# A decoder layer on one core: scale reciprocals moved from GpSimd to ScalarE, a correction product moved to the front of its group, and the second attention unit reordered

## The chip, the core and the metric

The kernel runs on one core of one Trainium2 chip. The metric is device microseconds of one execution. Before the change three runs took 1386.78, 1386.09 and 1386.69 us; the median is 1386.69. One further execution was recorded by the profiler, and every time of a single instruction below is from that record, counted from the start of its span.

The core has five engines with a queue each: PE (matrix products, into PSUM), DVE (VectorE), ACT (ScalarE), POOL (GpSimd) and SP, which here only issues DMAs. An engine works its queue in order. An instruction that waits holds up everything behind it on its engine.

## What is computed

One post-norm decoder layer on x of 8 sequences by 256 tokens by 512:

```python
x = layernorm(x + self_attention(x))        # 16 heads of 128, rotary, causal zeroing; weights sign(s)*exp(|s| - max|s|)
x = layernorm(x + cross_attention(x, ctx))  # 16 heads of 32, scores clipped to +-50, result scaled and normalised
x = layernorm(x + ffn(x))                   # 512 -> 2048 -> 512

def ffn(x):
    h = layernorm(gelu(bitlinear(x, w1, b1)))
    return bitlinear(h, w2, b2)

def bitlinear(x, w, b):
    # s = 127 / max(absmax of the row, 1e-5); xq = clip(round(x * s), -128, 127) / s
    # wq: weights rounded to -1, 0, 1 times their mean magnitude
    return xq @ wq.T + b
```

All of it is float32; the quantised products are made of small integers, times a scale for each row.

## The kernel before

**Self-attention.** The work is 32 units: 8 pairs of heads by 4 pairs of sequences. A float32 product is made of three PE products of a high and a low part (hi·hi, hi·lo, lo·hi: lines L146, L147 and L148). So every x and every weight is loaded into one of three buffers called `raw` and split: the high part is a copy (L156), and the low part a subtraction (L157, or L183 where the halves are made apart). What a unit does is written out by hand as a string of words, `SCHED["unit"]`. A word is one step of the unit's own projections (`Q` and `V` on PE; `w`, `u`, `r`, `R`, `H`, `L` for the rotation: L314 and L315 on ACT, `u` is L320 on DVE, L324 and L332 on POOL, `H` is L341 on ACT, `L` is L348 on POOL or DVE), of the unit before it (`s` to `l`: scores, mask, exponentials `x`, sums `n` and normalising `N`, the last being L411, L412 and the four L419 on DVE), or of the one before that (`o`, `d`: the output product). Other words run background work: `X0` splits the first half of the next unit's x on DVE, `XA` and `XB` make the high and the low part of its second half, `BA`, `BV`, `BW`, `BX`, `BY`, `G0` and `G1` load and split weights. All engines receive the steps in the order of the string; PE's order alone is left to a scheduler after unit 0. The second unit (number 1) has the string with a few replacements, since its predecessor and the loads stand differently: L633 to L637. A `raw` buffer is loaded again only when the split that reads it has run, so the place of `X0` in the string also sets when SP can issue the load of the x after that.

**Cross-attention, its norm and the FFN.** From L640 on the work is a list of steps. Each has an engine (or a choice), a cost and the tiles that it reads and writes; a planner puts the steps in order by these costs, and all queues are emitted in that order. The tokens are 16 tiles of 128. For each tile, after the cross-attention's output product (PE, tile `xo`):

- two norms; `rstd` (L763) makes 1/sqrt(v + eps) from a variance in two POOL instructions, L764 and L765 (the latter with a power of -1/2), and `shift` (L768) on DVE reads it;
- L980 on ACT writes the normed tile; `absmax` (L985 to L987) on DVE finds the row's largest magnitude and the reciprocal of its scale;
- `inverse` on POOL: eight small instructions. L993 writes `a1s`, the row scale that the gelu needs later; L994 clears the fifth block of the quantised tile `xq`; L996 multiplies the reciprocal with the weights' scale, and L999 and L1001 split that number into three bfloat16 parts, which are put into the fifth block (so that the bias can be added by a product);
- L1004 on ACT rounds the tile, by adding and so dropping digits; L1008 on DVE writes it to `xq`;
- SP transposes `xq` by DMA to `xT` (L1010) and stores that; it is loaded back as `xx` (L1060, a DMA that ACT issues) for the first FFN product (`up`, L1070 and L1071 on PE).

The FFN of a tile: the gelu L1075 on ACT, a square for the variance (L1084), three small POOL steps (L1089 to L1091), the second norm in halves (L1103 on ACT, L1105 or POOL for the gamma, L1107 on POOL for the beta, L1108 on DVE), the row's largest magnitude (L1111), then `scale` (L1116 to L1118): the larger of two halves' maxima, its floor and scale, and the reciprocal. ACT or DVE write the quantised `hq` (L1124, L1125), with one half added to make the numbers whole; it is transposed by SP (L1153) or by PE, into `hT`. `down` makes 16 products of 128x512 with `hT` (L1131) and one of a constant with the weights' column sums (L1133), which takes the added half away again. y and the last norm follow (L1155, L764, L765, L768, L1160), and the store.

```python
def down(ks_):
    for k in ks_:
        nc.tensor.matmul(H[dn], H[hT][:, k], H["fw1"][:, 512 * k : 512 * k + 512], start=k == 0, stop=False)
    if 15 in ks_:
        nc.tensor.matmul(H[dn], unhalf, csum, start=False, stop=True)
```

The listing below has the functions that the diff touches.

Of the kernel before, what the change touches and what calls it, by code (L numbers as in the profile page):

```python
# [11 lines left out]
F32R = mybir.dt.float32r  # L12
# [20 lines left out]
EPS = 1e-5  # L33
# [45 lines left out]
def decoder_kernel(ctx: ExitStack, tc: tile.TileContext, a, out):  # L79
# [442 lines left out]
    def background(ui):  # L522
        u = units[ui]
        ex = {k: [] for k in ("B0", "BA", "BV", "BW", "BX", "BY", "XA", "XB", "X0", "X1", "G0", "G1", "BP", "WK", "WV")}
        if ui == 0:
            ex["WK"].append(lambda: load_first("wK"))
            ex["WV"].append(lambda: load_hp(0, "wV", first["wV"]))
        nx = units[ui + 1] if ui + 1 < len(units) else None
        if nx is not None and nx.hp == 0:
            if ui == 0:  # L530
                ex["BA"].append(nx.xload)
            ex["X0" if ui < 2 else "B0"].append(lambda: nx.xsplit(0))
            ex["XA"].append(lambda: x_half(nx.xt, nx.raws[1], 1, 0, nc.scalar))
            ex["XB" if ui > 1 else "X1"].append(lambda: x_half(nx.xt, nx.raws[1], 1, 1, nc.vector))
        elif nx is not None:
            ex["BA"].append(nx.load)
        if ui < 2:
            ex["BV" if ui else "BW"].append(units[ui + 2].xload)
        if u.hp == 0:
            ex["BA" if ui else "X1"].append(lambda: init_acc(u.bp))  # L540
            ex["BA" if ui else "X1"].append(lambda: nc.sync.dma_start(f32(xs[u.bp][:]), f32(u.xt[:])))
        if "wv" in late:
            ex["B0"].append(lambda raw=late.pop("wv"): load_hp(u.hp, "wV", raw["w"]))
        for n, hp, k1 in ([("wO", u.hp, "BW")] if ui else [], [] if ui > 1 else [("wO", 0, "BW")], [("wQ", u.hp + 1, "BW")], [("wK", u.hp + 1, ""), ("wV", u.hp + 1, "")])[u.bp]:
            if (ui or n == "wO") and hp < NHP:
                raws = {}
                ex["BV" if n == "wV" else "BA"].append(lambda n=n, hp=hp, raws=raws: raws.update(w=raw_load(a[n][hp])))
                if n == "wV":
                    late["wv"] = raws
                elif n == "wK":  # L550
                    def hi(raws=raws, hp=hp):
                        w = hw.setdefault(hp, {})["wK"] = T("w", [128, 2, 1024], F32R)
                        half_split(w[:, 0], w[:, 1], raws["w"], 0, nc.scalar)

                    def lo(raws=raws, hp=hp):
                        w = hw[hp]["wK"]
                        half_split(w[:, 0], w[:, 1], raws["w"], 1, nc.vector)

                    ex["G0"].append(hi)
                    ex["BX"].append(lo)  # L560
                else:
                    ex[k1].append(lambda n=n, hp=hp, raws=raws: load_hp(hp, n, raws["w"]))
        if ui in ABS:
            for j in range(2):
                i, rr = 2 * ABS.index(ui) + j, {}
                ex["BA"].append(lambda i=i, rr=rr: rr.update(w=wchunk(i // 8, i % 8)))
                ex[f"G{j}"].append(lambda i=i, rr=rr: wq_abs(rr["w"], i // 8, i % 8))
        if "r2" in late:
# [12 lines left out]
        if ui == len(units) - 2:  # L581
            ex["BA"].append(lambda: kv0.update(wk0r=raw_load(a["wkx"][:, 0:1024])))
            ex["BW"].append(lambda: kv0.update(wk0=split_w(kv0["wk0r"])))
        if ui == len(units) - 1:
            ex["BA"].append(lambda: kv0.update(cr=x_raws(a["ctxT"][0])))

            def ctx_split(i):
                if i == 0:
                    kv0["ctx"] = T("xt", [128, 2, 4, 512], F32R)
                x_split(kv0["ctx"], kv0["cr"][i], i, (nc.vector, nc.gpsimd)[i])  # L590

            ex["X0"].append(lambda: ctx_split(0))
# [38 lines left out]
    for ui, u in enumerate(units):  # L631
        spec = SCHED["unit" if ui else "first"]
        if ui == 1:  # L633
            for old, new in ((" N0 XB", ""), (" n0 m1", " n0 N0 m1"), ("Q000 s00 Q001", "Q000 Q001 s00"), (" S0 BA", " S0 BA f0- f2-"),
                             (" V0 v0", ""), (" t00", " V0 v0 t00")):
                assert old in spec
                spec = spec.replace(old, new, 1)  # L637
# [84 lines left out]
    def new(key):  # L722
        if key in made:
            return []
        made.add(key)
        return [key]
# [127 lines left out]
    def x(b):  # L854
# [80 lines left out]
        for qi in range(2):  # L935
# [29 lines left out]
            def scale1(m1=m1):  # L965
# [12 lines left out]
            S([("POOL-", 1.0, lambda m2=m2: rstd(H[m2]))], wr=[m2])  # L978
# [9 lines left out]

            S([("DVE", 0.85, absmax)], rd=[A], wr=[f"{m2}/s"])

            def inverse(tt=tt, m2=m2, xq=xq):
                s, xq = H[m2], H[xq]
                nc.gpsimd.tensor_tensor(a1s[:, tt : tt + 1], s[:, 10:11], wscale[:, 0:1], ALU.mult)  # L993
                nc.gpsimd.memset(xq[:, 512:640], 0.0)  # L994
                inv = s[:, 12:13]
                nc.gpsimd.tensor_tensor(inv, s[:, 11:12], wscale[:, 2:3], ALU.mult)  # L996
                for n in (3, 2, 1):
                    c0 = 512 + 33 * (3 - n)
                    nc.gpsimd.tensor_copy(xq[:, c0 : c0 + 32 * n - 31 : 32], inv.to_broadcast([128, n]))  # L999
                    if n > 1:  # L1000
                        nc.gpsimd.tensor_tensor(inv, inv, xq[:, c0 : c0 + 1], ALU.subtract)  # L1001

            S([("POOL-", 2.0, inverse)], rd=[f"{m2}/s"], wr=[f"{xq}/i", f"a1s:{tt}"], new=new(xq))
            S([("ACT", 0.71, lambda tt=tt, d=d, m2=m2: nc.scalar.activation(H[d], acc[:, tt], AF.Identity, bias=magic, scale=H[m2][:, 11:12]))],  # L1004
              rd=[A, f"{m2}/s"], wr=[d])
# [44 lines left out]
    def ffn(tt):  # L1050
# [62 lines left out]

        def scale():
            s = H[st]
            nc.vector.tensor_tensor(s[:, 8:9], s[:, 8:9], s[:, 9:10], ALU.max)  # L1116
# [10 lines left out]
        bank(dn)  # L1127

        def down(ks_):
            for k in ks_:  # L1130
                nc.tensor.matmul(H[dn], H[hT][:, k], H["fw1"][:, 512 * k : 512 * k + 512], start=k == 0, stop=False)  # L1131
# [293 lines left out]
```

## Time and profile before

| | |
|---|---|
| median of three runs | 1386.69 us |
| profiled execution | 1387.89 us |
| its span, first to last instruction | 1386.1 us |
| PE busy | 1346.7 us (97%) |
| DVE busy | 1091.8 us (79%) |
| ACT busy | 880.4 us (64%) |
| POOL busy | 782.0 us (56%) |
| mean granted PE clock | 0.992 |
| chain that ended last | PE 82%, DVE 10%, POOL 3%, ACT 2%, issue 2%, DMA 1% |

How to read it: the profiled execution lies 1.8 us above its span, and that part is outside of what the engines do. The busy time of an engine says how full it is over the whole, not in a stage; the table by windows gives the same for one stretch. In a timeline a row has the start, the busy time, the engine, the line, the operation, the tiles that it writes and reads, and, in brackets, the idle time just ahead of it with what ended it. PEclk is the share of the full TensorE clock that was granted.

The stages in time: self-attention to about 900 us, keys, values and cross-attention to about 1225, the FFN from there to the end; FFN products of the first tiles lie between the last tiles of the cross-attention.

### The profile page before, as it was taken

Reading aid. Unit: us, or ns where it says so; the run is one execution under the profiler, and the core shown is the slowest. Engines: PE = TensorE matmul, PEld = TensorE weight load, DVE = VectorE, ACT = ScalarE, POOL = GpSimd, SP = SyncE. Lnnn points to the kernel's source line nnn. Section 1 sums busy time; section 2 is a strip of 40 time slices with the busy share of each in tenths; the row PEclk is TensorE's granted clock in tenths of the full one; section 3 lists DMA queues with packets and bytes.
Section 4 is the critical chain, followed back from the end, with each engine's and each line's share of the span. In section 5 each row is a group of like instructions: output and inputs, shape, how many; then the busy total and the mean of one; then the engine's idle time right before and its main releaser. Section 6 shows DMA issues by size and latency. Waiting matters only on the chain.

```text
span 1386.1 us, 23778 instructions
## 1 busy us (share of the span) xinstructions
PE 1346.7 (97%) x8576; PEld 1081.0 (78%) x8576; DVE 1091.8 (79%) x2040; ACT 880.4 (64%) x1948; POOL 782.0 (56%) x985
## 2 busy tenths in 40 slices
PE   9899999999999999999999999999999999988896
PEld 7789988898889888998889888888667667543342
DVE  6877768778767888887877876868767877798997
ACT  4666776776776666666665666633644445576995
POOL 5656556656666666766665665525033324376764
PEclk9999999999999999999999999999999999999999
DMA  8442342234322244223422342225324424214453
GB/s 309 182 185 109 116 178 107 92 114 165 121 76 96 92 143 176 104 84 124 189 88 99 126 175 107 69 99 191 114 59 126 140 68 143 86 34 94 113 116 99
DMA packets 85046, 170.13 MB, mean 123 GB/s; under 512 B 47040, under 2 KB 57024, under 8 KB 80064
## 3 DMA queue, kind: packets, MB, share of 16 engines
q1 hardware_dynamic: 82624, 165.99, 35.1%
q10 hardware_dynamic: 2304, 2.62, 0.7%
q8 instruction: 68, 1.11, 0.3%
q14 instruction: 50, 0.41, 0.1%
HBM read 130.31 MB, written 27.79 MB: 114 GB/s over the span
## 4 chain that ended last, share of the span: by engine, by line
PE 82%; DVE 10%; POOL 3%; ACT 2%; issue 2%; DMA 1%; SPq 0%; POOLq 0%; ACTq 0%; DVEq 0%
PE ppj L146 12%; PE ppj L147 12%; PE ppj L148 12%; PE pz L146 3%; PE pz L148 3%; PE pz L147 3%; PE pwt L426 3%; PE sc L880 3%; PE den L911 2%; PE av L895 2%; PE ppo L146 2%; PE ppo L147 2%; PE ppo L148 2%; PE psc L376 2%; PE pz L449 2%
## 5 line engine op out<-in xcount | busy, mean ns | idle before, releaser
L324 POOL TENSOR_TENSOR sw<-sw,stab 128x512 f32<-128x512 f32 x128 | 170.2, 1329 | 101.5 <-ACT sw L315 101.0
L146 PE MATMUL ppj<-xt,w 128*128 128x512 f32 x528 | 209.0, 396 | 0.3 <-ACT xt L285 0.3
L147 PE MATMUL ppj<-xt,w 128*128 128x512 f32 x528 | 206.5, 391 | 1.0 <-DVE xt L157 0.4
L148 PE MATMUL ppj<-xt,w 128*128 128x512 f32 x528 | 206.2, 391 | 0.0
L146 PE MATMUL ppj<-w,xt 128*128 128x256 f32 (+1 forms) x528 | 157.2, 298 | 1.1 <-DVE u L320 1.1
L348 POOL TENSOR_TENSOR rh<-u,rh 128x512 fp32r<-128x512 f32 x64 | 97.6, 1526 | 99.8 <-PE ppj L148 88.2
L148 PE MATMUL ppj<-w,xt 128*128 128x256 f32 (+1 forms) x528 | 152.0, 288 | 0.0
L147 PE MATMUL ppj<-w,xt 128*128 128x256 f32 (+1 forms) x528 | 151.9, 288 | 0.0
L320 DVE SCALAR_TENSOR_TENSOR u<-ppj,bqk,ctab 128x512 f32<-128x512 f32 x128 | 95.5, 746 | 70.9 <-ACT sw L315 70.6
L314 ACT ACTIVATE sw<-ppj,bqk 64x512 f32<-64x512 f32 x128 | 87.8, 686 | 92.7 <-PE ppj L148 87.9
L332 POOL TENSOR_TENSOR u<-u,sw 128x256 f32<-128x256 f32 (+1 forms) x128 | 130.8, 1022 | 0.3 <-DVE u L320 0.2
L419 DVE SCALAR_TENSOR_TENSOR e<-aw,rd,sg 128x128 f32<-128x128 f32 (+1 forms) x256 | 126.3, 550 | 0.1
L148 PEld LDWEIGHTS ppj<-xt,w 128*128 128x128 f32 x528 | 99.2, 188 | 21.6 <-DVE w L183 0.4
L406 ACT ACTIVATE aw<-aw,nm 128x256 f32<-128x256 f32 (+1 forms) x256 | 113.2, 443 | 3.9 <-DVE nm L397 3.9
L391 POOL TENSOR_SCALAR_AFFINE_SELECT aw<-aw 128x256 f32<-128x256 f32 x128 | 59.9, 492 | 98.7 <-ACT aw L385 98.7
L453 ACT CAST z<-pz 128x512 fp32r<-128x512 f32 x64 | 37.6, 587 | 121.3 <-PE pz L449 121.3
L147 PEld LDWEIGHTS ppj<-xt,w 128*128 128x128 f32 x528 | 99.3, 188 | 17.9 <-DVE xt L183 0.8
L146 PEld LDWEIGHTS ppj<-xt,w 128*128 128x128 f32 x528 | 99.3, 188 | 17.1 <-ACT xt L285 0.7
L146 PEld LDWEIGHTS ppj<-w,xt 128*128 128x128 f32 x528 | 101.9, 193 | 2.0 <-DVE u L320 1.4
L147 PEld LDWEIGHTS ppj<-w,xt 128*128 128x128 f32 x528 | 102.0, 193 | 0.6
L148 PEld LDWEIGHTS ppj<-w,xt 128*128 128x128 f32 x528 | 101.7, 193 | 0.7
L385 ACT ACTIVATE aw<-psc 128x384 f32<-128x384 f32 x128 | 62.3, 487 | 60.6 <-PE psc L148 59.9
(283 smaller groups left out, 3937.0 us busy)
## 6 DMA issues: line engine op xcount, KB each, us to landing
xt<-xs SPq DMA_DIRECT2D x28, 2048.0 KB, 8.2
xs<-xt SPq DMA_DIRECT2D x4, 2048.0 KB, 12.9
raw<-w1T SPq DMA_DIRECT2D x16, 512.0 KB, 9.5
raw<-w2T SPq DMA_DIRECT2D x16, 512.0 KB, 9.6
acc<-xn SPq DMA_DIRECT2D x4, 1024.0 KB, 8.5
raw<-wO SPq DMA_DIRECT2D x8, 512.0 KB, 9.6
wq<-wqt SPq DMA_DIRECT2D x16, 256.0 KB, 2.4
kx<-ks SPq DMA_DIRECT2D x8, 512.0 KB, 4.9
```

The lines of the kernel that those rows point to most:

```text
L146: nc.tensor.matmul(ps, lh, rh, start=first, stop=False)
L147: nc.tensor.matmul(ps, lh, rl, start=False, stop=False)
L148: nc.tensor.matmul(ps, ll, rh, start=False, stop=last)
L314: nc.scalar.activation(sw[0:64], ps[64:128], AF.Identity, bias=bias[64:128])
L320: nc.vector.scalar_tensor_tensor(v3(u), v3(self.ps.pop((h, i))), self.bias(h, i), ctab.to_broadcast([128, 2, 256]), ALU.add, ALU.mult)
L324: nc.gpsimd.tensor_tensor(v3(sw), v3(sw), stab.to_broadcast([128, 2, 256]), ALU.mult)
L332: nc.gpsimd.tensor_tensor(u, u, sw, ALU.add)
L348: (nc.gpsimd if i else nc.vector).tensor_tensor(lo, u if i else u[:, :, 128:256], f32(hi), ALU.subtract)
L385: nc.scalar.activation(aw[:, h], sc3, AF.Abs, scale=1.0 / math.sqrt(DH))
L391: nc.gpsimd.affine_select(aw[:, :, blk], aw[:, :, blk], pattern=[[0, 2], [-1, 128]], compare_op=ALU.is_ge, fill=MASKED, base=0, channel_mu ...
L406: nc.scalar.activation(aw[:, h, blk], aw[:, h, blk], AF.Exp, bias=nm[:, h, i : i + 1], accum_out=rd[:, h, i : i + 1])
L419: nc.vector.scalar_tensor_tensor(e[:, h, blk], aw[:, h, blk], rd[:, h, i : i + 1], sg[:, h, blk], ALU.mult, ALU.mult)
```

## The change

Six edits:

1. The seven small POOL instructions of `inverse` (all but the clearing) become seven small ACT instructions, emitted right behind the rounding L1004. The clearing of `xq`'s fifth block stays on POOL and moves to the step of `rstd`. The planner's POOL step remains as an empty one with its cost, and the ACT step keeps the cost 0.71, so the order of all other work is as before.
2. `rstd`'s first instruction multiplies by 1.0 and adds epsilon, where it only added.
3. `scale` takes the maximum by an instruction with one tensor and a pointer to the other number, with the floor in it; the product with 1/127 is the next one.
4. `down` makes the correction product first.
5. Unit 1 has other replacements: `X0` goes from behind `R00` to behind `N1`; `x0` goes ahead of `H00`; `N0` and the second `u10` go ahead of `R01`, and `L00` behind `N0`; `XA` and `XB` come later (`XB` at `BY`).
6. In unit 1 the weight wO is split in two steps, the high part on ACT at `G1` and the low part on DVE at `BW`, where DVE did both at `BW`.

```diff
-            ex["XB" if ui > 1 else "X1"].append(lambda: x_half(nx.xt, nx.raws[1], 1, 1, nc.vector))
+            ex["XB" if ui > 1 else "BY" if ui else "X1"].append(lambda: x_half(nx.xt, nx.raws[1], 1, 1, nc.vector))
...
-                elif n == "wK":
+                elif n == "wK" or ui == 1:
...
-                    ex["G0"].append(hi)
-                    ex["BX"].append(lo)
+                    ex["G0" if n == "wK" else "G1"].append(hi)
+                    ex["BX" if n == "wK" else "BW"].append(lo)
...
-            for old, new in ((" N0 XB", ""), (" n0 m1", " n0 N0 m1"), ("Q000 s00 Q001", "Q000 Q001 s00"), (" S0 BA", " S0 BA f0- f2-"),
+            for old, new in ((" N0 XB", ""), (" L00 n0 m1", " n0 N0 L00 u10 m1"), (" H01 u10 R10", " H01 R10"), (" H00 x0 a11 XA", " x0 H00 a11"), (" R00 X0", " R00"), (" N1 X1", " N1 X0"),
+                             (" l0 k10 k11 BX", " XA l0 k10 k11 BX"), ("Q000 s00 Q001", "Q000 Q001 s00"), (" S0 BA", " S0 BA f0- f2-"),
...
-        nc.gpsimd.tensor_scalar(mv[:, 2:3], mv[:, 1:2], EPS, None, ALU.add)
+        nc.gpsimd.tensor_scalar(mv[:, 2:3], mv[:, 1:2], 1.0, EPS, ALU.mult, ALU.add)
...
+            def rstd_zero(m2=m2, xq=xq):
+                rstd(H[m2])
+                nc.gpsimd.memset(H[xq][:, 512:640], 0.0)
...
-            def inverse(tt=tt, m2=m2, xq=xq):
-                s, xq = H[m2], H[xq]
-                nc.gpsimd.tensor_tensor(a1s[:, tt : tt + 1], s[:, 10:11], wscale[:, 0:1], ALU.mult)
-                nc.gpsimd.memset(xq[:, 512:640], 0.0)
+            S([("POOL-", 2.0, lambda: None)], rd=[f"{m2}/s"], wr=[f"{xq}/i", f"a1s:{tt}"], new=new(xq))
+
+            def rounded(tt=tt, d=d, m2=m2, xq=xq):
+                s, s_xq = H[m2], H[xq]
+                nc.scalar.activation(H[d], acc[:, tt], AF.Identity, bias=magic, scale=s[:, 11:12])
                 inv = s[:, 12:13]
-                nc.gpsimd.tensor_tensor(inv, s[:, 11:12], wscale[:, 2:3], ALU.mult)
-                for n in (3, 2, 1):
-                    c0 = 512 + 33 * (3 - n)
-                    nc.gpsimd.tensor_copy(xq[:, c0 : c0 + 32 * n - 31 : 32], inv.to_broadcast([128, n]))
+                nc.scalar.activation(inv, s[:, 11:12], AF.Identity, scale=wscale[:, 2:3])
+                for c0, n in ((512, 3), (545, 2), (578, 1)):
+                    nc.scalar.copy(s_xq[:, c0 : c0 + 32 * n - 31 : 32], inv.to_broadcast([128, n]))
                     if n > 1:
-                        nc.gpsimd.tensor_tensor(inv, inv, xq[:, c0 : c0 + 1], ALU.subtract)
-
-            S([("POOL-", 2.0, inverse)], rd=[f"{m2}/s"], wr=[f"{xq}/i", f"a1s:{tt}"], new=new(xq))
...
+                        nc.scalar.activation(inv, s_xq[:, c0 : c0 + 1], AF.Identity, scale=-1.0, bias=inv)
+                nc.scalar.activation(a1s[:, tt : tt + 1], s[:, 10:11], AF.Identity, scale=wscale[:, 0:1])
+
+            S([("ACT", 0.71, rounded)], rd=[A, f"{m2}/s"], wr=[d])
...
-            nc.vector.tensor_tensor(s[:, 8:9], s[:, 8:9], s[:, 9:10], ALU.max)
-            nc.vector.tensor_scalar(s[:, 8:9], s[:, 8:9], EPS, 1.0 / 127.0, ALU.max, ALU.mult)
+            nc.vector.tensor_scalar(s[:, 8:9], s[:, 8:9], s[:, 9:10], EPS, ALU.max, ALU.max)
+            nc.vector.tensor_scalar(s[:, 8:9], s[:, 8:9], 1.0 / 127.0, None, ALU.mult)
...
+            if 0 in ks_:
+                nc.tensor.matmul(H[dn], unhalf, csum, start=True, stop=False)
             for k in ks_:
-                nc.tensor.matmul(H[dn], H[hT][:, k], H["fw1"][:, 512 * k : 512 * k + 512], start=k == 0, stop=False)
-            if 15 in ks_:
-                nc.tensor.matmul(H[dn], unhalf, csum, start=False, stop=True)
+                nc.tensor.matmul(H[dn], H[hT][:, k], H["fw1"][:, 512 * k : 512 * k + 512], start=False, stop=k == 15)
```

More of the change, by code (lines that the diff above doesn't have):

```diff
@@ L549, in background, with hi, lo @@
                     late["wv"] = raws
-                elif n == "wK":
-                    def hi(raws=raws, hp=hp):
-                        w = hw.setdefault(hp, {})["wK"] = T("w", [128, 2, 1024], F32R)
+                elif n == "wK" or ui == 1:
+                    def hi(raws=raws, hp=hp, n=n):
+                        w = hw.setdefault(hp, {})[n] = T("w", [128, 2, 1024], F32R)
                         half_split(w[:, 0], w[:, 1], raws["w"], 0, nc.scalar)
-                    def lo(raws=raws, hp=hp):
-                        w = hw[hp]["wK"]
+                    def lo(raws=raws, hp=hp, n=n):
+                        w = hw[hp][n]
                         half_split(w[:, 0], w[:, 1], raws["w"], 1, nc.vector)
-                    ex["G0"].append(hi)
-                    ex["BX"].append(lo)
+                    ex["G0" if n == "wK" else "G1"].append(hi)
+                    ex["BX" if n == "wK" else "BW"].append(lo)
                 else:
@@ L977, in x @@
                ("ACT", 2.1, lambda d=d, m2=m2, xq=xq: astats(H[d], H[m2], H[xq][:, 0:512]))], rd=[d], wr=[m2, f"{xq}/q"], new=[m2] + new(xq))
-            S([("POOL-", 1.0, lambda m2=m2: rstd(H[m2]))], wr=[m2])
+            def rstd_zero(m2=m2, xq=xq):
+                rstd(H[m2])
+                nc.gpsimd.memset(H[xq][:, 512:640], 0.0)
+            S([("POOL-", 1.0, rstd_zero)], wr=[m2])
             S([("DVE", 0.13, lambda m2=m2: shift(H[m2]))], wr=[m2])
@@ L989, in x @@
             S([("DVE", 0.85, absmax)], rd=[A], wr=[f"{m2}/s"])
-            def inverse(tt=tt, m2=m2, xq=xq):
-                s, xq = H[m2], H[xq]
-                nc.gpsimd.tensor_tensor(a1s[:, tt : tt + 1], s[:, 10:11], wscale[:, 0:1], ALU.mult)
-                nc.gpsimd.memset(xq[:, 512:640], 0.0)
+            S([("POOL-", 2.0, lambda: None)], rd=[f"{m2}/s"], wr=[f"{xq}/i", f"a1s:{tt}"], new=new(xq))
+            def rounded(tt=tt, d=d, m2=m2, xq=xq):
+                s, s_xq = H[m2], H[xq]
+                nc.scalar.activation(H[d], acc[:, tt], AF.Identity, bias=magic, scale=s[:, 11:12])
                 inv = s[:, 12:13]
-                nc.gpsimd.tensor_tensor(inv, s[:, 11:12], wscale[:, 2:3], ALU.mult)
-                for n in (3, 2, 1):
-                    c0 = 512 + 33 * (3 - n)
-                    nc.gpsimd.tensor_copy(xq[:, c0 : c0 + 32 * n - 31 : 32], inv.to_broadcast([128, n]))
+                nc.scalar.activation(inv, s[:, 11:12], AF.Identity, scale=wscale[:, 2:3])
+                for c0, n in ((512, 3), (545, 2), (578, 1)):
+                    nc.scalar.copy(s_xq[:, c0 : c0 + 32 * n - 31 : 32], inv.to_broadcast([128, n]))
                     if n > 1:
-                        nc.gpsimd.tensor_tensor(inv, inv, xq[:, c0 : c0 + 1], ALU.subtract)
-            S([("POOL-", 2.0, inverse)], rd=[f"{m2}/s"], wr=[f"{xq}/i", f"a1s:{tt}"], new=new(xq))
-            S([("ACT", 0.71, lambda tt=tt, d=d, m2=m2: nc.scalar.activation(H[d], acc[:, tt], AF.Identity, bias=magic, scale=H[m2][:, 11:12]))],
-              rd=[A, f"{m2}/s"], wr=[d])
+                        nc.scalar.activation(inv, s_xq[:, c0 : c0 + 1], AF.Identity, scale=-1.0, bias=inv)
+                nc.scalar.activation(a1s[:, tt : tt + 1], s[:, 10:11], AF.Identity, scale=wscale[:, 0:1])
+            S([("ACT", 0.71, rounded)], rd=[A, f"{m2}/s"], wr=[d])
             S([(e, us, lambda tt=tt, g=g: g.tensor_tensor(acc[:, tt], acc[:, tt], H["b2b"], ALU.add))
```

## The prediction, made before the changed kernel had run

> **What bounds the kernel now.** I read the table by windows first, because the page's 97% for PE is a mean over stages with different limits.
>
> ```profile
> core 0: us, PE busy (x) PEld busy (x) DVE busy (x) ACT busy (x) POOL busy (x), PEclk, DMA share, GB/s
> 0.00:40.00 40.00, 36.52 (x189) 30.28 (x190) 26.50 (x44) 18.29 (x31) 22.69 (x24) 1.00 0.85 306
> 40.00:80.00 40.00, 36.17 (x205) 31.59 (x204) 32.48 (x60) 29.39 (x80) 26.96 (x29) 0.91 0.33 119
> 80.00:900.00 820.00, 819.68 (x5023) 732.87 (x5022) 644.64 (x1222) 545.97 (x1435) 516.17 (x541) 1.00 0.33 124
> 1200.00:1250.00 50.00, 43.77 (x250) 23.30 (x242) 43.11 (x81) 34.90 (x51) 31.27 (x63) 0.93 0.16 40
> 1250.00:1300.00 50.00, 41.91 (x179) 17.72 (x179) 43.87 (x75) 36.89 (x44) 33.43 (x41) 0.93 0.46 102
> 1300.00:1350.00 50.00, 47.39 (x219) 21.08 (x218) 49.31 (x89) 48.41 (x60) 33.80 (x43) 1.00 0.53 115
> ```
>
> From 80 to 900 us PE is busy 819.68 of 820 us (and 298.33 of 300 from 900 to 1200): whatever is gained before 80 us is kept, and whatever ACT, DVE or POOL spares inside is worth nothing unless a PE row waits for it. The places to gain are the two stretches with PEclk 0.91 and 0.93, and the end, where DVE is busy 49.31 of 50. DVE's own waits from 1276 to 1373 sum to 0.9 us, so DVE time saved there counts in full.
>
> Unit 1 is the first stretch. In PE's timeline the fourth column is the idle time before a row and its releaser:
>
> ```profile
> 44.05 0.33 PE L426 MATMUL pwt<-ident,e 128*128 128x128 f32 x1 [1.57 <-DVE e L419]
> 44.59 0.44 PE L426 MATMUL pwt<-ident,e 128*128 128x128 f32 x2 [0.21 <-DVE e L419]
> 45.86 0.83 PE L426 MATMUL pwt<-ident,e 128*128 128x128 f32 x3 [0.83 <-DVE e L419]
> 47.84 0.58 PE L146 MATMUL ppj<-w,xt 128*128 128x256 f32 x1 [1.15 <-DVE u L320]
> 48.22 0.42 PE L147 MATMUL ppj<-w,xt 128*128 128x256 f32 x1
> ```
>
> PE waits 1.57 + 0.21 + 0.83 + 1.15 = 3.76 us for DVE, and then its clock falls: 26 matmuls of 256 columns start 0.214 us apart, against 0.119 elsewhere, (0.214 - 0.119) x 26 = 2.5 us more. The stretch loses 6.3 us. DVE is late because it splits unit 2's x just before; its subtraction L157 is stretched:
>
> ```profile
> 36.40 0.86 DVE L156 CAST xt<-raw 128x1024 fp32r<-128x1024 f32 x1
> 37.30 2.20 DVE L157 TENSOR_TENSOR xt<-raw,xt 128x1024 fp32r<-128x1024 f32 x1
> 39.42 0.74 DVE L320 SCALAR_TENSOR_TENSOR u<-ppj,bqk,ctab 128x512 f32<-128x512 f32 x1
> ```
>
> The second place is the start of the FFN. The chain of waits there:
>
> ```profile
> 1247.98 1.27 POOL a1s L993
> ...
> 1249.76 0.56 POOL xq L999
> ...
> 1250.39 1.19 POOL mb L1001
> ...
> 1252.16 0.20 POOL xq L999
> 1252.38 2.57 DMA xT<-xq
> 1254.97 0.32 SPq L1011
> 1255.39 4.32 DMA hT<-hq
> 1259.75 6.37 PE dn L1131 x16
> ...
> 1274.12 2.12 DVE fs L1116
> ```
>
> POOL's tiny operations on 128x1 take up to 1.27 us instead of 0.19. The last release the xT transposes on SP, the first hT transpose waits in SP's queue behind them, and PE is idle 4.77 us before dn, which then runs at half clock (6.37 us, against 3.63 at 1375.69).
>
> **Unit 1 reordered.** X0 (0.86 + 2.20 on DVE) leaves its place ahead of L320 of u01 (39.42) and goes behind N1; the second u10 comes before R01; L00 goes behind N0. Walking the new order with each row's own duration: u01 at 37.7 (not 39.42), H00 39.5, the four L419 39.95 to 42.25 (before 43.45 to 46.2), u10 42.55 to 43.25 (before 47.05 to 47.78). The projection that started at 47.84 can start at 43.3. What is late next: its second group wants L348 of L01 on POOL, about 47.0 (1.55 us idle); the third waits for u11 (0.5); unit 2's first projection waits for X0, now 52.2 to 54.1 (0.45), and XB's subtraction, now behind w's high half, 56.15 to 57.4 (0.7); with small ones of 1.0 that is 4.2 us idle, but spread over 15 us. The 12th matmul of unit 2 ends at 58.5 instead of 61.1: **-2.6 us**. Bounds: if the clock falls anyway, +1.7, so -0.9; if the L348 wait vanishes too, -6. A loss is possible by one DMA: unit 3's first raw load needs X0's buffer, so its issue on SP moves from 39.52 to 54.2. Its landing took 3.8 us then and 7.3 to 11.4 for other raw loads of the stage; it lands at 58 to 65.6, wanted by DVE at about 60. Behind it in SP's queue stand the second raw load, acc, xs and wQ, none wanted before 70. At worst 5 us are lost here, net +2.5.
>
> wO's high half goes from DVE (0.68) to ACT (1.04): the walk holds it, and ACT has 10 us idle of 40 there.
>
> **Reciprocals to ACT.** Each of 16 tiles takes seven small operations off POOL (0.32 + 0.30 + 0.28 + 0.31 + 0.31 + 0.31 + 0.28 = 2.1 us mean, 2.5 with gaps) and puts seven behind L1004 on ACT. L758 to L761 show a small ACTIVATE at 0.19 to 0.20, and a pointer operand at 0.1 (L757 0.62 with none, L759 0.72 with one, L1004 0.82 with two). Four with one pointer, three without, six of them dependent with 0.04 between: 4 x 0.29 + 3 x 0.19 + 6 x 0.04 - overlap of the last, 0.2 = 1.7 us. I take **1.6 per tile**; bounds 1.3 (no pointer price) and 2.0. No table is loaded for it.
>
> What stands behind them on ACT decides. The place to read it is tile 5:
>
> ```profile
> 1103.58 0.82 ACT L1004 ACTIVATE d<-acc,magic,mb 128x512 f32<-128x512 f32 x1 [1.19 <-DVE mb L987]
> 1104.31 0.67 ACT L845 ACTIVATE qst<-qp,bqx 128x512 f32<-128x512 f32 x1
> 1104.88 1.93 ACT L884 ACTIVATE pt<-sc 128x1024 f32<-128x1024 f32 x2
> ```
>
> L845 starts as L1004 ends, the two exps follow it, and the score matmuls L880 at 1106.73 have 0.05 us of slack to them: PE loses up to 1.6. Tile 7 has 0.86 us of ACT idle behind it and then an exp with 0.29 of slack (loss 0.5); tile 9, 0.2. Tiles 0, 1, 6 and 8 have gaps of 1.31 to 4.63 us; tiles 2 and 4 have PE slacks of 1.45 and 1.48 against delays of 0.8 and 1.4. So 1.6 + 0.5 + 0.2 = 2.3, less some slack that returns: **+2.0**, bounds 0 and +5 (a delay passing on through PE at tiles 2, 4, 10 and 11 too).
>
> At the FFN, ACT is full from 1238.8 to 1249.3, so tile 15's L1004 moves from 1247.36 to 1248.9 (1.6 for tile 14's burst before it), its parts are ready at 1251.1, not 1252.36, and xT, hT and dn come 1.2 us earlier. L1107 (two times 2.4 us on POOL, now from 1252.31 because the tiny operations stand before it) can start near 1246; DVE's wait of 3.04 at 1251.6 goes with it, but what it feeds waits for ACT's gelus, 1.6 late each. I take **-1.5** for both, bounds +3.2 (two bursts in full) and -5.
>
> **L1116.** The two-operand max took 2.19 us at 1274.04, against a median of 0.15, because POOL's L1107 ran from 1272.88 to 1276.21. In that same time DVE's L768, one operand with a pointer, took 0.20 at 1273.91. The new max has L768's form: 2.19 - 0.16 = **-2.0** at a point from where DVE is saturated. Bounds 0 (still held) and -2.7 (with the 0.65 at 1234.51).
>
> The Trainium skill, "SBUF — State Buffer", section "SBUF: two separate sides", says that a VectorE instruction with two SBUF inputs and a GpSimd one lock each other out for a whole instruction. By that rule the new form runs free whenever POOL runs; L768's 0.20 agrees. The same rule would free DVE from the seven operations on POOL as well, and nothing in my sum counts that. The skill's "ScalarE: Activation LUTs", section "What ACT_TABLE_LOAD costs", speaks against the change: 186 ns for an ACTIVATE and 93 more per pointer operand, so by estimate 4 x 0.28 + 3 x 0.19 = 1.69 us a tile, where my sum has 1.6; by the page the tile 5 loss would be 0.1 more.
>
> **down and rstd.** The correction product goes ahead of the 16 matmuls that wait for hT; the last of these releases y instead of L1133 (1379.32, 0.23 us). Other tiles are DVE-bound: **-0.3**, bounds 0 and -1. rstd keeps its instructions (L764 0.33, L967 with two operations 0.36): 0, bounds ±0.3. The moved memset (0.2) stays on POOL behind L765, and delays DVE's shift by nothing, as that waits for L765 alone.
>
> **Sum**, against the profiled 1387.89 us (span 1386.1 and 1.8 around it): -2.6 + 2.0 - 1.5 - 2.0 - 0.3 = -4.4, giving 1383.5. The profiled execution is 1.2 above the median, so 1386.69 - 4.4 = **1382.3** on the median's scale.
>
> **The rivals.**
> - Larger gain: the idle in unit 1 is spread, so the clock stays up and L348 comes sooner (-5), the FFN's start gives its best (-5), the middle costs 0.5: -10 to -12, about 1376. For it: every loss I named rests on slacks under 1.6 us. Against: POOL is already 27 of 40 busy in unit 1.
> - No change: the clock falls in unit 1 (-0.9), the middle costs 3, L1116 is held by another POOL operation (-1), the start of the FFN gives -1: about 0, 1386.7.
> - **Slower**: ACT becomes the bound at the FFN's start. Tiles 12 to 15 each put 1.6 us into ACT's queue, which has 1.35 us of idle behind tile 13's L1004 and none from 1238.8 to 1249.3; if gelu L1075 releases DVE and PE last, 4 x 1.6 - 1.35 = 5 us come in, DVE's saturated stretch starts later by 5 - 1.5, and with +2 in the middle, -2.6 from unit 1 and nothing else gained it is +3: 1390. It decides once the gelus delay dn more than the earlier transposes advance it, that is over 2.7 us. Against it: hT's transpose, not a gelu, released PE at 1259.75.
>
> **How the numbers follow.** About 0.2% (2.8 us) is what a measurement of this kernel tells from no change. Chances: forecast 0.46 (1379 to 1383.9), larger gain 0.16, no change 0.19, slower 0.19. So faster 0.62, same 0.19, slower 0.19. The forecast, the no-change case and most of the larger gain must be inside for 8 in 10, and the unknown bounds reach both: 1375.5 to 1388.5.
>
> **What would show it.** Right: PE's 47.84 row at 43 to 44 us and 256-column matmuls 0.12 apart; L1116 all at 0.2; xT's last landing and dn near 1251 after the shift, DVE busy over 49 of 50 to the end. Wrong: PE idle behind L884 of 0.5 us or more at more than three tiles; a DMA as releaser at 60 us; PE's wait before the first dn above 4.8 us with an ACT row as its releaser.

## The result, and the profile after

The changed kernel takes 1394.14 us (median of 6 runs, 1393.39 to 1394.68), against 1386.74 for the kernel before in its 6 runs: a ratio of 1.0053, interval 1.0040 to 1.0066. It is slower by some 7.4 us. Its profiled execution took 1393.39 us with a span of 1391.5. The forecast was 1382.3, with 1388.5 as the upper end.

Line numbers of the changed kernel lie one higher at L764 to L975 (L802 is L803), four or five higher around the rounding (L980 is L985, L1006 is L1010; the rounding itself, L1004, is L1000) and four in most of the FFN (L1060 is L1064, L1107 is L1111, L1116 is L1120). The kernels of the experiments have numbers of their own, off by a few lines; the names of the tiles tell the rows.

Where it went is read by stage. To make the two traces comparable I follow PE's instructions, which come in the same order in both but for the first stage, and note by how much each starts later than before. The shift is -1.1 to -1.3 us from unit 2 to 960 us, -1.7 from 990 to 1056, +0.6 after 1058, +2.1 after 1108, +2.5 after 1150, +2.9 at 1204; then comes the FFN's start, with almost +9 at its worst, and +5.4 is left at the end. The table by windows has the same (the columns are those of the table in the prediction):

```profile
core 0: us, PE busy (x) PEld busy (x) DVE busy (x) ACT busy (x) POOL busy (x), PEclk, DMA share, GB/s
...
1000.00:1100.00 100.00, 98.09 (x820) 68.88 (x821) 73.99 (x136) 51.59 (x99) 28.14 (x46) 1.00 0.31 98
1100.00:1200.00 100.00, 98.35 (x897) 65.93 (x899) 70.51 (x131) 60.34 (x114) 23.81 (x44) 1.00 0.38 116
1200.00:1250.00 50.00, 41.05 (x264) 22.99 (x265) 42.07 (x79) 38.94 (x77) 23.39 (x38) 0.97 0.12 31
```

PE was busy 100.00 and 99.72 of the first two windows before; it now has 1.9 and 1.6 us of idle time in a stage where all of it counts. ACT went from 44.39 and 54.36 to 51.59 and 60.34, and POOL from 36.62 and 36.61 to 28.14 and 23.81: the move happened as planned, and neither engine is near full.

The stall near 1057 us. The kernel before comes first, with a DVE, a POOL and a PE row; the bracket is the idle time ahead of the row and what ended it:

```profile
1053.07 0.69 DVE L985 TENSOR_REDUCE mb<-acc 128x1 f32<-128x512 f32 x1 [0.28 <-ACT acc L980]
...
1055.42 0.69 DVE L785 CAST ctx<-cr 128x1024 fp32r<-128x1024 f32 x1
1056.43 0.69 DVE L802 TENSOR_TENSOR kvs<-kvp,bvb 128x512 f32<-128x512 f32 x1 [0.33 <-POOL mb L1001]
```

```profile
1056.63 1.27 POOL L1006 TENSOR_TENSOR acc<-acc,b2b 128x512 f32<-128x512 f32 x1
```

```profile
1057.34 0.50 PE L146 MATMUL kvp<-w,ctx 128*128 128x512 f32 x1
```

The changed kernel, DVE, POOL and PE:

```profile
1053.17 0.69 DVE L990 TENSOR_REDUCE mb<-acc 128x1 f32<-128x512 f32 x1 [2.05 <-ACT acc L985]
...
1055.53 1.75 DVE L786 CAST ctx<-cr 128x1024 fp32r<-128x1024 f32 x1
1057.20 0.68 DVE L803 TENSOR_TENSOR kvs<-kvp,bvb 128x512 f32<-128x512 f32 x1
```

```profile
1055.23 1.50 POOL L1010 TENSOR_TENSOR acc<-acc,b2b 128x512 f32<-128x512 f32 x1 [2.95 <-ACT d L1000]
```

```profile
1057.93 0.50 PE L146 MATMUL kvp<-w,ctx 128*128 128x512 f32 x1 [1.91 <-DVE kvs L803]
```

Two things delay L803, which frees a PSUM bank for PE. ACT's L985 of the next tile stands behind a burst, so DVE waits 2.05 us where it waited 0.28. And the cast L786, now beside POOL's L1010, takes 1.75 us; before, it took 0.69 here and at 1048.22. PE, which did not wait here before, waits 1.91.

The stall near 1107 us is the one that the prediction named (tile 5), first on ACT, then on PE. Before, the score products ran without a wait:

```profile
1106.73 1.26 PE L880 MATMUL sc<-qst,kx 32*128 32x256 f32 x16
```

In the changed kernel:

```profile
1104.62 0.28 ACT L1002 ACTIVATE mb<-mb,wscale 128x1 f32<-128x1 f32 x1
...
1106.20 0.29 ACT L1007 ACTIVATE a1s<-mb,wscale 128x1 f32<-128x1 f32 x1
1106.39 0.67 ACT L846 ACTIVATE qst<-qp,bqx 128x512 f32<-128x512 f32 x1
1106.96 1.93 ACT L885 ACTIVATE pt<-sc 128x1024 f32<-128x1024 f32 x2
```

```profile
1108.03 0.70 PE L881 MATMUL sc<-qst,kx 32*128 32x256 f32 x4 [0.64 <-ACT pt L885]
```

From L1002 to L846 it is 1.77 us: the seven. PE comes out 1.5 us later.

At the FFN's start the chain of waits no longer goes through POOL's tiny operations. It goes through ACT's burst and then through two DVE rows, and by several short steps to a load of xx:

```profile
1249.99 0.82 ACT acc L985
...
1254.49 2.75 DVE acc L1010
...
1257.31 3.22 DVE h L1112
...
1269.08 3.21 DMA xx<-xqs
...
1272.34 1.89 PE up L1074 x4
```

PE waits 5.16 us for that load. L985 is again the next tile's norm behind a burst. L1010 and L1112 are ordinary additions, which took 0.67 and 1.27 us before. POOL's pair of additions lies beside them. It starts later than before (1252.31), because it waits for a DVE row that stands behind L985:

```profile
1254.23 5.21 POOL L1111 TENSOR_TENSOR h<-h,be 128x1024 f32<-128x1024 f32 x2 [3.75 <-DVE h L1109]
```

### The profile page after: what moved, and what is told of

The parts are those of the page before. It is cut to its first block, busy times and chain, and to the rows that moved or that the text cites. A ratio compares the mean times of both kernels' runs of the same rounds, so it can differ in the third digit from the quotient of the medians.

```text
span 1391.5 us, 23789 instructions
## 1 busy us (share of the span) xinstructions
PE 1347.6 (97%) x8564; PEld 1080.5 (78%) x8576; DVE 1093.8 (79%) x2039; ACT 905.2 (65%) x2061; POOL 750.7 (54%) x873
## 5 line engine op out<-in xcount | busy, mean ns | idle before, releaser
L348 POOL TENSOR_TENSOR rh<-u,rh 128x512 fp32r<-128x512 f32 x64 | 97.5, 1523 | 98.3 <-PE ppj L148 88.2
L419 DVE SCALAR_TENSOR_TENSOR e<-aw,rd,sg 128x128 f32<-128x128 f32 (+1 forms) x256 | 127.1, 554 | 0.1
```

Of the source, the lines that this page charges most:

```text
L348: (nc.gpsimd if i else nc.vector).tensor_tensor(lo, u if i else u[:, :, 128:256], f32(hi), ALU.subtract)
L419: nc.vector.scalar_tensor_tensor(e[:, h, blk], aw[:, h, blk], rd[:, h, i : i + 1], sg[:, h, blk], ALU.mult, ALU.mult)
```

## The experiments

The theories, stated before the first of them. **A, burst**: the seven ACTIVATEs hold up what stands behind them on ACT. **B, collision**: POOL, with the small work gone, runs its large additions sooner, at times when DVE needs the same memory. **C**: another of the edits costs it. The kernel before was timed again beside each; its median was 1386.9 to 1387.6.

**All edits but the first.**

```diff
-            S([("POOL-", 2.0, lambda: None)], rd=[f"{m2}/s"], ...)   # and the seven in rounded()
+            S([("POOL-", 2.0, inverse)], rd=[f"{m2}/s"], ...)        # as before
```

> All edits but the first: the seven small operations of a tile are POOL's again. Theory A (burst): the seven ACTIVATEs behind the rounding hold up what stands behind them on ACT, about 1.6 us a tile, and cost some 9 us; the rest of the change gains 1 to 2.5. Theory B (collision): POOL, freed of the seven, runs its 128x512 and 128x1024 operations at times when DVE needs the same memory, and this costs the 9 us. Theory C: another edit (the correction product first, the new maximum) costs it. A and B: 1384 to 1386. C: 1390 or more.

1384.99 us, ratio 0.9985 (0.9975 to 0.9994). C falls: the rest of the change is a gain of about 2 us.

**The first edit alone**, that is the hunks on `rstd_zero`, `inverse` and `rounded`.

```diff
-            S([("POOL-", 2.0, inverse)], rd=[f"{m2}/s"], ...)
+            S([("POOL-", 2.0, lambda: None)], rd=[f"{m2}/s"], ...)   # and the seven in rounded()
```

> The kernel before with the first edit alone (seven small operations of a tile from POOL to ACT). A and B: 1394 to 1397, PE waiting about 2.0 us near 1057 us and 1.5 near 1107, as in the changed kernel. C: 1386 to 1388.

1396.60, ratio 1.0067 (1.0052 to 1.0082): 9.6 us more. With the gain of the rest that makes 7.6, beside the 7.4 of the whole change. PE waits 1.9 us for L802 near 1057 and 0.8 for the exponentials, as in the changed kernel.

**POOL freed, burst left out.** Against the kernel with the first edit alone:

```diff
                 nc.scalar.activation(H[d], acc[:, tt], AF.Identity, bias=magic, scale=s[:, 11:12])
-                inv = s[:, 12:13]
-                nc.scalar.activation(inv, ...)   # and the three copies and two differences
                 nc.scalar.activation(a1s[:, tt : tt + 1], s[:, 10:11], AF.Identity, scale=wscale[:, 0:1])
```

> The kernel before with POOL freed, but ACT gets one small operation a tile (the row scale for the gelu) and not seven: the three bfloat16 parts of the reciprocal are left out, so the FFN's first bias is not added. POOL is as free as in the changed kernel, ACT's burst is 0.3 us and not 1.7. A: 1385 to 1388. B: 1391 or more, with the cast of ctx at 1057 us stretched to 1.7 us and PE waiting behind it.

1390.07, ratio 1.0021 (1.0011 to 1.0031): 3.0 us more, between the two expectations. One ACTIVATE of 0.28 us a tile is still on ACT, so the 3.0 is the freed POOL's cost together with that one's.

**Burst added, POOL not freed.**

```diff
                 nc.scalar.activation(H[d], acc[:, tt], AF.Identity, bias=magic, scale=s[:, 11:12])
+                a_, b_ = s[:, 13:14], s[:, 14:15]
+                nc.scalar.activation(a_, s[:, 11:12], AF.Identity, scale=wscale[:, 2:3])
+                for n in (3, 2, 1):
+                    nc.scalar.copy(b_, a_)
+                    if n > 1:
+                        nc.scalar.activation(a_, b_, AF.Identity, scale=-1.0, bias=a_)
+                nc.scalar.activation(s[:, 15:16], s[:, 10:11], AF.Identity, scale=wscale[:, 0:1])
```

> The kernel before, with seven more small ACTIVATEs of the same kinds behind each rounding, written to unused columns; POOL keeps its own seven. ACT has the burst and POOL is not freed. A: 1393 to 1396. B: 1386 to 1389. If each has a part: both this and the kernel without the parts lie between 1387 and 1393, and their excesses add up to that of the first edit alone.

1393.14, ratio 1.0046 (1.0031 to 1.0061): 6.1 us more. So A is the larger part by the medians, B is real, and 6.1 + 3.0 = 9.1 beside the 9.6 of both together. The place near 1057 us shows the two apart. DVE with the burst alone:

```profile
1053.04 0.69 DVE L985 TENSOR_REDUCE mb<-acc 128x1 f32<-128x512 f32 x1 [1.99 <-ACT acc L980]
...
1055.38 0.69 DVE L785 CAST ctx<-cr 128x1024 fp32r<-128x1024 f32 x1
```

DVE with POOL freed alone, and POOL beside it:

```profile
1051.65 0.69 DVE L989 TENSOR_REDUCE mb<-acc 128x1 f32<-128x512 f32 x1 [0.47 <-ACT acc L984]
...
1054.01 1.77 DVE L785 CAST ctx<-cr 128x1024 fp32r<-128x1024 f32 x1
```

```profile
1053.72 1.52 POOL L1003 TENSOR_TENSOR acc<-acc,b2b 128x512 f32<-128x512 f32 x1 [1.38 <-ACT d L999]
```

The burst gives the wait and a cast of 0.69. Freed POOL gives hardly a wait, but its addition, which before began 1.2 us after the cast did, now lies over it, and the cast takes 1.77. PE waits 0.8 us in the one, 0.6 in the other, and 1.9 with both. At the FFN's start the same is seen larger. DVE before, then with POOL freed alone, then POOL in that kernel:

```profile
1249.58 0.67 DVE L1006 TENSOR_TENSOR acc<-acc,b2b 128x512 f32<-128x512 f32 x1
1250.25 1.27 DVE L1108 SCALAR_TENSOR_TENSOR h<-h,fs,be 128x1024 f32<-128x1024 f32 x1
...
1254.68 2.35 DVE L1111 TENSOR_REDUCE fs<-h 128x1 f32<-128x1024 f32 x2 [3.04 <-POOL h L1107]
```

```profile
1249.33 2.85 DVE L1003 TENSOR_TENSOR acc<-acc,b2b 128x512 f32<-128x512 f32 x1
1252.17 3.30 DVE L1105 SCALAR_TENSOR_TENSOR h<-h,fs,be 128x1024 f32<-128x1024 f32 x1
```

```profile
1249.16 5.23 POOL L1104 TENSOR_TENSOR h<-h,be 128x1024 f32<-128x1024 f32 x2 [2.42 <-DVE h L1102]
```

POOL's pair of additions starts at 1249.16, not 1252.31: 3.1 us sooner, half of the some 6 that were forecast. But DVE's two additions now lie beside it and pay 2.18 + 2.03 = 4.2 us, and what DVE saves is its wait of 3.04.

A freed POOL is not the only way to such a meeting. With the burst alone DVE comes later to the second addition, and there it meets POOL's pair too, first the DVE row, then the POOL row:

```profile
1254.17 3.43 DVE L1119 SCALAR_TENSOR_TENSOR h<-h,fs,be 128x1024 f32<-128x1024 f32 x1
```

```profile
1254.18 5.62 POOL L1118 TENSOR_TENSOR h<-h,be 128x1024 f32<-128x1024 f32 x2
```

So 6.1 and 3.0 tell the two edits apart, but not waiting from collision: part of the burst's 6.1 is a collision as well.

**Where on the way: the first twelve tiles, and the last four.** The first edit is made for one part of the tiles only.

```diff
+            if tt < 12:      # tt >= 12 in the other
+                S([("ACT", 0.71, rounded)], ...)                   # the seven on ACT
+            else:
                 S([("POOL-", 2.0, inverse)], ...)                  # the seven on POOL
```

> The kernel before with the first edit at the tiles 0 to 11 alone (those that lie beside the cross-attention's products, where PE is busy throughout); the last four tiles keep the seven operations on POOL. The prediction's share for these tiles: 2.0 more, 1389.5. By the trace of the first edit alone, PE is 6.1 later at 1201 us than before: if that is kept to the end, 1393 to 1394; if the waits of the FFN's start (10 us of idle PE in 1226 to 1260) absorb it, 1388 to 1390.

> The kernel before with the first edit at the tiles 12 to 15 alone, those that the FFN's start waits for. The prediction's share for these: 1.5 less, 1386.0. If the burst holds up the next tile's norm on ACT and the gelus here, and POOL's 128x1024 additions meet DVE's two-tensor operations: 2.5 to 5 more, 1390 to 1392.5. The two shares add up to the 9.6 of the whole edit if neither absorbs the other.

1393.15, ratio 1.0044 (1.0029 to 1.0059), 6.3 us more; and 1389.93, ratio 1.0022 (1.0012 to 1.0031), 3.1 us more. Together 9.4: the shares add up, and nothing of a delay from before the FFN is absorbed at its start. In the first of them PE's waits from 1226 us on are those of before (hT 10.2 us, xx 7.3), only later. Its trace also shows what a wait can draw after it. PE's shift grows by 6.2 us from 1054 to 1225, against 4.7 in the changed kernel's trace. Both have the wait of 1.91 at 1057. But with the first twelve tiles alone the granted clock is then 0.72 from 1057 to 1063 (that is 3.4 us at half clock), against 1.00 in the changed kernel, and PE loses 1.6 us more there. The trace of the first edit alone has that spell too (0.74). In how many of the other executions it came, the record doesn't show.

**The same burst, later on ACT.** It is emitted with the step of L1012.

```diff
-            S([("ACT", 0.71, rounded)], ...)    # rounding and the seven
+            S([("ACT", 0.71, rounded)], ...)    # rounding
...
+            S([("DVE+", 0.36, store)], ...)     # L1012's step, and the seven on ACT
```

> The changed kernel with the same seven ACTIVATEs a tile, emitted with the step that stores the quantised tile, so that one to three other ACT instructions of the same plan go ahead of them: the next tile's norm at the second and third tile (near 1057 us), an exponential or the next scale elsewhere, a gelu at the FFN's start; at the tile near 1107 us the exponentials stay behind them. If the cost is in what stands behind the burst: PE's wait near 1057 falls from 1.9 to the 0.6 that the freed POOL alone shows, the 1.5 near 1107 stays, 1389 to 1392.5. If 1.6 us more on ACT cost the same wherever they stand: 1393 to 1395.

1392.65, ratio 1.0036 (1.0024 to 1.0048). Near 1057 PE waits 0.85 and not 1.91; near 1107 it still loses 1.5; against the kernel before it is 5.1 us more, where the changed kernel is 7.4, a difference that the two intervals do not separate. The places moved as A says; the sum says little.

**xx loaded by SP**, since ACT issued one such load at 1249.61, behind a burst, and PE waited 5.1 us for it.

```diff
-        S([("SP", 0.9, lambda: nc.scalar.dma_start(H[x2], xqs[tt]))], ...)
+        S([("SP", 0.9, lambda: nc.sync.dma_start(H[x2], xqs[tt]))], ...)
```

> The changed kernel with the loads of xx issued by SP, not ACT. In the changed kernel ACT issues the load at 1249.61 behind a burst, and PE waits 5.1 us for it. If that is what makes the FFN's start late: 3 us or more less, 1391 or below. If the start is late by ACT's queue itself (the next tile's norm L985 behind the burst, DVE behind that): within 1.5 of the changed kernel's 1394, though PE's wait for xx is another.

1393.88, ratio 1.0045 (1.0032 to 1.0059): 6.3 us more, no gain that the intervals tell from the changed kernel's 1.0053. PE's wait at that place falls to 0.3 us and comes back at the next (3.0, 2.9). Who issues the load was not what made the stage late.

**The seven on DVE**, at the end of the step with the row's maximum, and none on ACT.

```diff
                 nc.vector.reciprocal(s[:, 11:12], s[:, 10:11])
+                nc.vector.tensor_scalar(inv, s[:, 11:12], wscale[:, 2:3], None, ALU.mult)
+                for c0, n in ((512, 3), (545, 2), (578, 1)):
+                    nc.vector.tensor_copy(s_xq[:, c0 : c0 + 32 * n - 31 : 32], inv.to_broadcast([128, n]))
+                    if n > 1:
+                        nc.vector.tensor_tensor(inv, inv, s_xq[:, c0 : c0 + 1], ALU.subtract)
+                nc.vector.tensor_scalar(a1s[:, tt : tt + 1], s[:, 10:11], wscale[:, 0:1], None, ALU.mult)
```

> The changed kernel with the seven small operations on DVE, at the end of the step that finds the row's maximum, and none on ACT. POOL is freed as in the changed kernel. ACT's burst is gone and its 6 us with it; what the freed POOL costs (3 us) stays, and DVE gets some 1.4 us a tile. If DVE hides them as ACT could not, since it has 26 of 100 us idle from 1000 to 1200: 1386 to 1389. If a burst of this length hurts on any engine ahead of the copies that PE waits for: 1391 to 1396.

1397.13, ratio 1.0070 (1.0056 to 1.0084): 9.6 us more, no better than on ACT. In the changed kernel DVE has 26 us idle of 100, but here PE waits for its masked exponentials, its kvs, rs and cT (0.3 to 0.7 us at five places before 1201 us; it is 4.5 later there), and the FFN's start adds 5 more. An idle quarter is no cover when what PE needs next stands right behind.

**The order planned anew.**

```diff
-            S([("POOL-", 2.0, lambda: None)], ...)
...
-            S([("ACT", 0.71, rounded)], rd=[A, f"{m2}/s"], wr=[d])
+            S([("ACT", 2.3, rounded)], rd=[A, f"{m2}/s"], wr=[d, f"{xq}/i", f"a1s:{tt}"], new=new(xq))
```

> The changed kernel, with the planner told of the burst: the empty POOL step is gone, and the rounding step has a cost of 2.3 instead of 0.71, so the order of all engines behind it is planned anew. If the burst hurts by standing ahead of exponentials, gelus and loads that an ignorant plan put right behind it, a plan that knows it gets half of it or more back: 1385 to 1390. If the 1.6 us a tile on ACT hurt wherever they stand: 1392 to 1396.

1502.06, ratio 1.0825: neither. The new plan changes between exponentials and gelus, with 8 loads of a function table at 1.28 us each where there were 2, and PE waits 32 us for hT. It tells how much the order of the plan is worth, and nothing on the burst.

**The other edits one by one**, each with the kernel before around it. First the maximum.

```diff
-            nc.vector.tensor_tensor(s[:, 8:9], s[:, 8:9], s[:, 9:10], ALU.max)
+            nc.vector.tensor_scalar(s[:, 8:9], s[:, 8:9], s[:, 9:10], EPS, ALU.max, ALU.max)
```

> The kernel before with the new maximum alone. L1116 takes 0.2 us everywhere. The prediction's step: DVE is the bound from there on, so 2.0 us less, 1385.0. Rival: DVE comes to y 2 us sooner and waits there for the second dn, whose time its transpose and PE set: 0 to 0.6 less, 1386.4 to 1387.0.

1385.66, ratio 0.9988 (0.9979 to 0.9996). The row that took 2.19 us before, with POOL's addition beside it as it was before:

```profile
1272.24 0.20 DVE L1116 TENSOR_SCALAR fs<-fs 128x1 f32<-128x1 f32 x1
```

```profile
1271.09 3.35 POOL L1107 TENSOR_TENSOR h<-h,be 128x1024 f32<-128x1024 f32 x1 [1.65 <-DVE h L1105]
```

The second unit (edits 5 and 6 of the list).

```diff
-            for old, new in ((" N0 XB", ""), (" n0 m1", " n0 N0 m1"), ...)
+            for old, new in ((" N0 XB", ""), (" L00 n0 m1", " n0 N0 L00 u10 m1"), ...)
```

> The kernel before with the second unit reordered and wO split in two steps, nothing else. The prediction's step: 2.6 us less, 1384.4 against 1387.0. What the changed kernel's trace says (0.7 us less idle, a half-clock stretch shorter by part of a window, which differs between executions by itself): 0.5 to 1.3 us less, 1385.7 to 1386.5.

1386.58, ratio 0.9995 (0.9986 to 1.0004): 0.8 us less, not told from no change.

The correction product and `rstd` (edits 4 and 2).

```diff
+            if 0 in ks_:
+                nc.tensor.matmul(H[dn], unhalf, csum, start=True, stop=False)
```

> The kernel before with the correction product first and the other form of the variance's first step. The prediction's step: 0.3 us less, 1386.7. If the sum of the edits is what the kernel without the parts shows (2.0 less), the three parts of it, this one, the new maximum and the second unit, add up to 2.0.

1386.49, ratio 0.9994 (0.9986 to 1.0003): 0.8 less, not told from no change either; by the traces DVE's rows lie 0.2 us sooner than before at 1200 and 0.5 sooner from 1282 on. The three together make 3.3, with intervals of some 1.2 each, beside the 2.0 of the kernel that has all three.

**A shorter chain on POOL**, with all edits but the first.

```diff
             def rstd_zero(m2=m2, xq=xq):
                 rstd(H[m2])
+                nc.gpsimd.memset(H[xq][:, 512:640], 0.0)      # out of inverse
...
                         nc.gpsimd.tensor_tensor(inv, inv, xq[:, c0 : c0 + 1], ALU.subtract)
+                nc.gpsimd.tensor_tensor(a1s[:, tt : tt + 1], s[:, 10:11], wscale[:, 0:1], ALU.mult)   # was first
```

> The kernel with all edits but the first, with the clearing of the fifth block moved to the step of the variance and the gelu's row scale put last, so that the parts of the reciprocal are ready two POOL instructions sooner. POOL's work is the same. Before, these two were 1.7 us of the chain at 1243 to 1250. If they hold up the transposes: 0.3 to 1.5 less than the 1385.0 of the kernel without the parts, 1383.5 to 1384.7. If the transposes are late for other reasons: 1385 to 1386.

1384.80, ratio 0.9982 (0.9973 to 0.9991). It beats both kernels, and is the same as the one without the parts (0.9985) within the intervals: that the transposes wait for these two instructions isn't shown.

## Why the prediction was wrong, point by point

- **Reciprocals to ACT, price of the burst: right.** 1.6 us a tile was taken, 1.77 measured, with 0.28 to 0.30 for a small ACTIVATE with one pointer, 0.20 for a copy and 0.03 to 0.08 between dependent ones. The terms of the prediction's own sum add up to 1.77; it wrote 1.7 and then took 1.6. The figures of the Trainium skill, "ScalarE: Activation LUTs", section "What ACT_TABLE_LOAD costs" (186 ns, and 93 for each pointer) agree.
- **What stands behind it, before the FFN: the step that failed in size.** The prediction took +2.0 for tiles 0 to 11, with +5 as the upper bound, and 6.3 was measured. The price at tile 5 was right (1.6 forecast, 1.5 seen), and at tile 7 (0.5, 0.5 seen). Tile 2 was not: I gave it a PE slack of 1.45 against a delay of 0.8, which holds for the exponentials. The way that mattered goes from ACT's L980 of the next tile by DVE's absmax, which DVE works in order, to L802 behind it and to the PSUM bank that L802 frees. There PE had hardly 0.2 us (L802 ended at 1057.12, PE's row began at 1057.34). The spell at half clock that can follow the wait, 1.6 us in the traces that have it, was no term either. I followed who waits for the burst on ACT, and not who stands behind the waiting instruction on DVE.
- **The FFN's start, -1.5: wrong sign.** The last four tiles alone cost 3.1. The forecast moved tile 15's rounding by the 1.6 us of tile 14's burst and had the first dn 1.2 sooner. But the rounding also needs tile 15's norm, which stands behind the same burst, and DVE's maximum of it: with the last four tiles alone it started at 1249.46 and not 1247.36, the first dn at 1260.08 and not 1259.75, and PE then waited 5.05 for xx. The other half was POOL's L1107, whose earlier start I counted as a gain of up to 3.04 us. With POOL freed alone it came sooner and DVE lost 4.2 beside it; in the changed kernel the burst held it until 1254.23, and DVE's two additions lay beside it all the same (2.83 and 3.29 us).
- **What was left out of the sum: POOL's new times, 3 us.** Every price of the prediction is a row's duration in the profile before, so each contains which POOL instruction happened to run beside it. Moving POOL's work moves those meetings. The rule of the Trainium skill, "SBUF — State Buffer", section "SBUF: two separate sides", stood in the prediction as a relief for DVE only. It works the other way too: a cast of 128x1024, without a second operand, went from 0.69 to 1.77, and an addition from 0.67 to 2.85. The page's two conditions (a 2-port mode, two SBUF inputs), of which the prediction named only the second, fit these rows, though no run here shows which mode the cast was in.
- **Unit 1, -2.6: 0.8 measured, interval from 1.9 less to 0.6 more.** The walk failed at the same point. It gave the four L419 2.3 us, though their row before has 2.75; after the change they meet more of POOL's rotation and take 3.69:

```profile
39.42 1.16 DVE L411 TENSOR_SCALAR rd<-rd 128x4 f32<-128x4 f32 x1 [1.14 <-ACT aw L406]
...
40.83 3.69 DVE L419 SCALAR_TENSOR_TENSOR e<-aw,rd,sg 128x128 f32<-128x128 f32 x4
```

  PE's projection starts at 45.58 where I had 43.3 (47.84 before). PE's own rows:

```profile
42.91 0.44 PE L426 MATMUL pwt<-ident,e 128*128 128x128 f32 x2 [0.49 <-DVE e L419]
44.19 0.83 PE L426 MATMUL pwt<-ident,e 128*128 128x128 f32 x3 [0.84 <-DVE e L419]
45.58 0.39 PE L146 MATMUL ppj<-w,xt 128*128 128x256 f32 x1 [0.56 <-DVE u L320]
```

  The clock still fell, for half as long as before, and what came is close to the prediction's bound for that case, -0.9. The raw load that moves on SP did no harm: PE has no wait for it.
- **L1116, -2.0: right.** 1.7 us less, interval 0.6 to 2.9. The rival that I put beside it before its run, that dn would eat the gain, was wrong for the edit alone; in the changed kernel the gain of 1.98 at that row is followed by a wait of 1.53 for dn, since PE is later there.
- **down and rstd, -0.3: within the interval** of -1.9 to +0.4.
- **The slower rival** put the loss at the FFN's start by ACT alone and at +3 in all. It named ACT rightly, but at the last four tiles alone, and nothing of POOL's part.

Not settled: how the 3 us of the freed POOL divide over its places. At 1057 us 0.7 shows on PE and at the FFN's start 1.2 net on DVE; in its profiled execution PE falls from 0.9 to 2.8 us late at the end, beside a dn of 6.54 us (3.63 before) at half clock, which I can't tell from chance.

## What to carry to other kernels

A duration taken from a profile belongs to the neighbours that it had. When work leaves an engine that shares a path to memory with another, list what will now run sooner there and beside which instructions; a freed POOL, with one small instruction left on ACT, cost 3 us here. When a burst is put on an engine with idle time, follow what stands behind it on that engine and then what stands behind the waiter on the next one: 1.8 us on an engine that was half idle cost 6 us, because a saturated PE was waiting two queues on.

## What the runs showed of the hardware

The time at half clock in unit 1 comes in equal pieces. In all eight profiled executions without the reordering the granted clock is 0.83 from 40 to 60 us, that is 6.8 us at half; in seven of eight with it 0.91, that is 3.4; in the eighth, the second unit alone, 1.00. That fits the window of 3413 ns that the Trainium skill states in "TensorE: Matmul & The Clock Gate", section "What's actually happening", but in the changed kernel the drop came after 0.49 + 0.84 + 0.56 = 1.89 us of idle time in three pieces within 3.2 us, not after a whole idle window. And it did not matter: from 30 to 100 us the eight with the reordering gain 0.93 to 0.96 us against the profile before, the one without a half-clock spell too, because PE then waits 0.90 for POOL's L348 instead. The other seven executions without it, whose kernels differ in nothing here, spread from +0.02 to -0.94 over the same stretch. A comparison of two profiles cannot price a step of less than 1 us there.
